# Second attention of a four-layer network: output biases moved to the projections, scales issued slot by slot, variance constant folded into the root, states copied by whole banks

## The chip, the core and the metric

The kernel runs on one core of one Trainium2 chip. The metric is the device time of one execution in microseconds; the median of three runs stands for a kernel. Five engines work beside each other, each through its own instructions in order: PE (TensorE, matrix products), DVE (VectorE), ACT (ScalarE), POOL (GpSimd) and SP, which here only issues DMAs. All data are float32.

## The reference

The network has four layers over 4096 tokens of 256 channels. Layers 0 and 1 are convolutional; layer 2 has the attention that the change touches, followed by a mixture of eight experts with two chosen for each token; layer 3 is softmax attention and again a mixture of experts. The attention of layer 2, with eight heads of h = 32 channels, is

```
q, k, v = linear(x)                                 # x: layer norm of t
sim  = sum(q * k) * qk_norm_scale
k, v = k / |k|, v / |v|
Z    = outer(v, k) * kv_norm_scale                  # h x h for each token and head
gates = square(relu(Z.flat @ wg.T + wg_b)) + 1e-5
m, s  = online softmax scan of sim                  # running maximum and sum
Z_scan, g_scan = cumsum(gates * Z), cumsum(gates)
weights = exp(sim - m) / (s + 1e-5)
attn = Z_scan / (g_scan + 1e-5) * (1 + silu(weights))
t = t + linear(q @ attn, wo_w, wo_b)
```

so the sum over earlier tokens is linear attention, and each token and head has one factor, (1 + silu(weights)) / (g_scan + 1e-5), which can be put on q. The layer norm divides by sqrt(var + 1e-5); the router of the experts works on a second layer norm of the new t.

## The kernel before

Tokens lie on the 128 partitions: 32 tiles (NT) of 128 tokens, 8 blocks (NBLK) of 4 tiles (TPB), 16 slots of 2 tiles. `attn2` (L1375) runs in three stages.

**Projections** (`attn2_project`, L1466 on), one set of steps for each block: `norm` (layer norm of t into a_n), `turn` (transposes on PE), four times `project` (products on PE, bias added by DVE at L1492 into a_qk and a_v), `lengths` (squares on ACT, sums on DVE, the product q*k on POOL at L1502), `sims`, `turn_v`, and `gates` (products with wg on PE, then a row of DVE operations L1524 to L1532, and on POOL at L1533 the keys times their gate). The loop in `attn2` calls them so that block b's gates stand beside block b+1's projections and block b+2's norm. Only PE follows that written order; the instructions of the other engines are ordered by the framework's scheduler, which takes what is ready by its own estimate of time. The projections of one block are 32 matmuls.

**Factors** (`attn2_fac`, L1560). The order of PE, DVE, ACT and POOL is written out by hand. Gates and sims are turned so that 256 values of one head and slot range lie along the free axis; the scans run on DVE; `carry` (L1592) takes the ends of the rows through two small products (a_c and a_back) to give each row its start. It is called twice, for sums and maxima and then for the softmax total. Between these, `beside(n)` issues n of the 31 products of the states (`attn2_states`, L1539): for a tile, 8 small products v by k into one of four PSUM banks (a_st_ps), and after every fourth tile a copy by ACT (L1554) of four states into SBUF and then four running sums by POOL (L1556). The total's reciprocal is L1645, Silu L1647, the reciprocal of the gates' sum L1648, both put together by L1649; PE turns the result (L1653) and DVE copies it to a_fac (L1654).

**Slots** (`attn2_sum`, L1656), also in hand-written order on four engines. For slot u: `scale` (POOL, L1671) multiplies q by the factor, `turn` (PE, copied by ACT at L1682) transposes q, `scores` (PE L1692, masked by DVE at L1695), `context` (PE: L1706 with the states of earlier tiles, L1712 within the tile; ACT L1725 copies), and `out` for the slot before (PE, then DVE adds the product to t at L1731). `bias` (POOL, L1674) adds wo_b to t. All scales and biases are queued on POOL before the loop over slots. The routing for the experts (`route_parts`, L2020 on) is woven into the loop: for four tiles each, statistics of t (DVE L212, L213), the root of the variance (`norm_parts`, `root`), `scales` (L222, L225, L2042), the normed rows (ACT L232, and POOL L2046 for one column), transposes (L2051), logits, the two best experts, places, and the scattering of rows by indirect DMAs that POOL issues (L2103). The first route has its statistics in slots 1 and 2, its root in slot 2 and its scatters in slots 6 and 7.

`norm_parts` (L201) makes the root with two instructions, which all layer norms of the attention and of the routing use:

```
nc.vector.tensor_scalar_add(r, mv[:, :, 1], eps)    # L217
nc.scalar.activation(r, r, AF.Sqrt)                 # L218
```

Of the kernel before, what the change touches and what calls it, by code (L numbers as in the profile page):

```python
# [10 lines left out]
F32 = mybir.dt.float32  # L11
# [77 lines left out]
class Net:  # L89
# [6 lines left out]
    def constants(self, pool):  # L96
        nc = self.nc
        self.ident = pool.tile([P, P], F32, tag="ident", name="ident")
        make_identity(nc, self.ident)
        self.ones_row = pool.tile([1, P], F32, tag="ones_row", name="ones_row")  # L100
        nc.gpsimd.memset(self.ones_row, 1.0)
        self.one = pool.tile([P, 1], F32, tag="one", name="one")
        nc.gpsimd.memset(self.one, 1.0)
        self.ones_col = self.one

        self.flags = pool.tile([P, 3], F32, tag="flags", name="flags")
# [94 lines left out]
    def norm_parts(self, pool, x, out, eps, on_act):  # L201
# [13 lines left out]
        def root():  # L215
            r = got["r"] = room("ln_rstd")
            nc.vector.tensor_scalar_add(r, mv[:, :, 1], eps)  # L217
            nc.scalar.activation(r, r, AF.Sqrt)  # L218
# [1156 lines left out]
    def attn2(self, t, S):  # L1375

        nc, tc = self.nc, self.tc
        with tc.tile_pool(name="a2", bufs=1) as pool:
# [16 lines left out]
            with (  # L1395
# [20 lines left out]
            A["st"] = left.enter_context(tc.tile_pool(name="a2s", bufs=1)).tile([P, NT, 2, D], F32, tag="st", name="a2_st")  # L1416
            self.attn2_fac(A)
            with (
# [12 lines left out]
                self.attn2_sum(t, A, tri, ked, wp, ps, route)  # L1431
# [33 lines left out]
    def attn2_project(self, b, t, A, wg_bd, wp, ps):  # L1465
# [47 lines left out]

        def turn_v():
# [21 lines left out]
        return {"norm": norm, "turn": turn, "lengths": lengths, "sims": sims, "turn_v": turn_v, "gates": gates,  # L1536
                **{i: call(i) for i in range(TPB)}}

    def attn2_states(self, A, ps):  # L1539
# [5 lines left out]
        def product(ti):  # L1545
# [6 lines left out]
            if ti % 4 == 3 or ti == NT - 2:  # L1552
                lo = ti // 4 * 4
                nc.scalar.copy(st[:, lo + 1 : ti + 2], banks[-1][:, lo % 8 : ti % 8 + 1])  # L1554
                for i in range(max(1, lo), ti + 1):
                    nc.gpsimd.tensor_tensor(st[:, i + 1], st[:, i + 1], st[:, i], ALU.add)  # L1556

        return [(lambda ti: lambda: product(ti))(ti) for ti in range(NT - 1)]

    def attn2_fac(self, A):  # L1560
# [5 lines left out]
        with (  # L1566
# [4 lines left out]
            states = self.attn2_states(A, ps)  # L1571

            def beside(n):
                for go in states[:n]:
                    go()
                del states[:n]
# [15 lines left out]
            def carry(ends, scan, first, fill):  # L1592
# [14 lines left out]
                beside(1)  # L1607
# [12 lines left out]
            def sums_and_tops(x, c):  # L1620
# [3 lines left out]
            c2 = carry([ends[:, 0:1], ends[:, 1:2]], sums_and_tops, (0.0, -3e38), 8)  # L1624
# [12 lines left out]
            nc.vector.tensor_scalar_add(gs, gs, 1e-5)  # L1637
            tot = pool.tile([P, L], F32, tag="tot", name="a2_tot")
# [3 lines left out]
                       (0.0,), 12)  # L1642
# [5 lines left out]
            nc.vector.reciprocal(gs, gs)  # L1648
            nc.vector.scalar_tensor_tensor(s, s, 1.0, gs, ALU.add, ALU.mult)  # L1649
            beside(len(states))  # L1650
# [3 lines left out]
            nc.vector.tensor_copy(A["fac"].rearrange("p a s h -> p a (s h)"), p)  # L1654

    def attn2_sum(self, t, A, tri, ked, wp, ps, route):  # L1656
# [15 lines left out]

        def bias(u):
            nc.gpsimd.tensor_tensor(t[:, two(u), :], t[:, two(u), :], bc(self.row("wo_b"), 1, 2), ALU.add)  # L1674
# [66 lines left out]
        with self.tc.manual_schedule(engines={ET.PE, ET.DVE, ET.Activation, ET.Pool}):  # L1741
            scale(0)
            scale(1)
            bias(0)
            turn(0)
            scores(0)
            for u in range(2, U):
                scale(u)
                bias(u - 1)
            bias(U - 1)  # L1750
            for u in range(U + 6):
                if u + 1 < U:
                    turn(u + 1)
# [1160 lines left out]
```

## Time and profile before

| | us |
|---|---|
| runs | 3508.52, 3509.21, 3514.0 |
| median | 3509.21 |
| profiled execution | 3443.01 |
| its span, first to last instruction | 3441.5 |
| layers 0 and 1, start of the second attention's loads | 0 to 1433.4 |
| projections | 1433.4 to 1570.7 |
| factors | 1570.7 to 1590.7 |
| slots, with the routing's tail | 1590.7 to 1762.3 |
| experts, third layer's attention and experts, output | 1762.3 to 3441.5 |

Busy shares of the span: PE 90%, DVE 67%, ACT 39%, POOL 42%; the mean granted clock of PE is 0.951. A line of the profile gives the start and length in us (or, for groups, the count, the busy time and the mean in ns), the engine, the line of the kernel, the operation, what it writes and reads, and in brackets how long its engine had been idle and what ended the wait. "L146" is the helper for matrix products, so the tile's name tells which product it is. Digits are left out of tile names (a2_st is a_st). The engine's order is that of its queue: an instruction that waits holds up all behind it.

### The profile page before, as it was taken

Reading aid. Unit: us, or ns where it says so; the run is one execution under the profiler, and the core shown is the slowest. Engines: PE = TensorE matmul, PEld = TensorE weight load, DVE = VectorE, ACT = ScalarE, POOL = GpSimd, SP = SyncE. Lnnn points to the kernel's source line nnn. Section 1 sums busy time; section 2 is a strip of 40 time slices with the busy share of each in tenths; the row PEclk is TensorE's granted clock in tenths of the full one; section 3 lists DMA queues with packets and bytes.
Section 4 is the critical chain, followed back from the end, with each engine's and each line's share of the span. In section 5 each row is a group of like instructions: output and inputs, shape, how many; then the busy total and the mean of one; then the engine's idle time right before and its main releaser. Section 6 shows DMA issues by size and latency. Waiting matters only on the chain.

```text
span 3441.5 us, 66218 instructions
## 1 busy us (share of the span) xinstructions
PE 3103.2 (90%) x25772; PEld 2319.7 (67%) x25772; DVE 2311.1 (67%) x5339; ACT 1327.2 (39%) x2554; POOL 1457.5 (42%) x1323
## 2 busy tenths in 40 slices
PE   6779999999977899896969789999999996999997
PEld 3443444344436888665857567888888885999996
DVE  8885777577754677796855576777777775555552
ACT  4444334444425666242633352222222222333331
POOL 2028788778843555326344352000000003555552
PEclk9889999999988999897979899999999997999998
DMA  2146556521134222100158643323333214555554
GB/s 74 40 114 142 161 154 168 130 68 52 48 116 111 68 74 73 44 1 2 52 183 264 215 181 127 98 86 98 99 99 98 91 64 154 200 194 199 206 206 176
DMA packets 241688, 407.01 MB, mean 118 GB/s; under 512 B 78353, under 2 KB 152850, under 8 KB 231890
## 3 DMA queue, kind: packets, MB, share of 16 engines
q1 hardware_dynamic: 212002, 344.40, 32.2%
q0 software_dynamic: 13056, 35.93, 2.8%
q10 hardware_dynamic: 16304, 22.31, 1.9%
q8 instruction: 207, 3.39, 0.4%
q14 instruction: 119, 0.97, 0.1%
HBM read 287.07 MB, written 111.30 MB: 116 GB/s over the span
## 4 chain that ended last, share of the span: by engine, by line
PE 42%; DVE 9%; DMA 5%; issue 5%; ACT 3%; POOL 3%; SPq 0%; POOLq 0%; DVEq 0%; ACTq 0%
PE a_sa_ps L2537 6%; PE f_h_ps L146 5%; DMA ys<-f_y,f_at 3%; PE l_acc_ps L1154 3%; PE a_oa_ps L2576 3%; PE a_ob_ps L2576 3%; PE a_oc_ps L2576 3%; PE a_sb_ps L2537 3%; PE f_ya_ps L146 2%; PE f_yb_ps L146 2%; POOL ys L2292 2%; DVE l_pr L1150 2%; PE a_od_ps L2576 1%; PE a_q_ps L146 1%; PE a_qkv_ps L146 1%
## 5 line engine op out<-in xcount | busy, mean ns | idle before, releaser
L770 ACT COPY l_sc<-l_s 128x384 f32<-128x384 f32 (+1 forms) x632 | 304.0, 532 | 456.9 <-PE l_s L763 445.0
L775 DVE TENSOR_TENSOR l_sm<-l_s,mask 128x256 f32<-128x256 f32 (+2 forms) x628 | 308.2, 552 | 89.2 <-PE l_s L763 88.0
L2103 POOL DMA_INDIRECT xs<-f_room,f_to x64 | 64.5, 1007 | 698.0 <-issue 582.4
L146 PE MATMUL f_h_ps<-f_xT,f_w 128*128 128x256 f32 x1440 | 341.1, 388 | 19.4 <-DVE f_xT L2212 9.7
L146 PEld LDWEIGHTS f_h_ps<-f_xT,f_w 128*128 128x128 f32 x1440 | 262.2, 192 | 84.0 <-ACT f_h L2222 31.3
L763 PE MATMUL l_s<-l_q,l_k 32*128 32x256 f32 (+3 forms) x2944 | 270.5, 453 | 0.0
L2556 ACT ACTIVATE a_e<-a_e 128x512 f32<-128x512 f32 x256 | 156.0, 629 | 246.2 <-DVE a_e L2526 245.2
L780 POOL TENSOR_TENSOR l_sm<-l_sc,mask 128x768 f32<-128x768 f32 (+1 forms) x116 | 201.9, 1748 | 88.2 <-ACT l_sc L770 88.1
L2222 ACT ACTIVATE f_h<-f_h_ps,f_w 128x256 f32<-128x256 f32 x360 | 166.6, 470 | 187.9 <-PE f_h_ps L146 178.7
L1150 DVE TENSOR_TENSOR l_pr<-l_vk,l_w_ps 128x1280 f32<-128x1280 f32 x128 | 186.7, 1482 | 55.2 <-PE l_acc_ps L1154 37.6
L763 PEld LDWEIGHTS l_s<-l_q,l_k 32*128 32x128 f32 x2944 | 132.4, 183 | 115.2 <-issue 67.5
L2292 POOL DMA_INDIRECT ys<-f_y,f_at x144 | 145.7, 1012 | 140.6 <-ACT f_y L2291 110.0
L1154 PE MATMUL l_acc_ps<-ident,l_pr 128*128 128x128 f32 x1600 | 198.1, 278 | 7.7 <-POOL l_pr L1145 7.6
L1154 PEld LDWEIGHTS l_acc_ps<-ident,l_pr 128*128 128x128 f32 x1600 | 184.7, 144 | 14.1 <-POOL l_pr L1145 8.3
L784 POOL TENSOR_TENSOR l_sm<-l_sc,mask 128x256 f32<-128x256 f32 (+1 forms) x220 | 184.9, 868 | 16.1 <-ACT l_sc L770 15.2
L2249 POOL TENSOR_TENSOR f_wt<-f_w 128x512 f32<-128x512 f32 x72 | 89.8, 1268 | 217.1 <-PE f_ya_ps L146 204.9
L2537 PE MATMUL a_sa_ps<-a_q,a_kt 128*128 128x256 f32 x512 | 155.6, 386 | 15.1 <-DVE a_u L2542 14.3
L2541 ACT COPY a_u<-a_sa_ps 128x256 f32<-128x256 f32 x128 | 47.6, 372 | 292.0 <-PE a_sa_ps L2537 292.0
L809 PE MATMUL l_b_ps<-l_sm,l_v 128*32 128x256 f32 (+2 forms) x2176 | 153.7, 372 | 0.0
L2537 PE MATMUL a_sa_ps<-a_qt,a_kt 128*128 128x256 f32 x512 | 152.3, 379 | 0.0
L780 POOL TENSOR_TENSOR l_sm<-l_sc,mask_c 128x768 f32<-128x768 f32 (+1 forms) x64 | 122.9, 1937 | 39.7 <-ACT l_sc L770 39.2
L2537 PE MATMUL a_sb_ps<-a_qt,a_kt 128*128 128x256 f32 x512 | 131.4, 379 | 0.0
(558 smaller groups left out, 7292.1 us busy)
## 6 DMA issues: line engine op xcount, KB each, us to landing
a_kt<-a_kd SPq DMA_DIRECT2D x128, 512.0 KB
f_w<-in_f_w SPq DMA_DIRECT2D x36, 1152.0 KB
f_w<-in_f_w SPq DMA_DIRECT2D x36, 1028.0 KB
xs<-zero SPq DMA_DIRECT2D x8, 4160.0 KB
l_vk<-vt SPq DMA_DIRECT2D x180, 128.0 KB
f_x<-xs SPq DMA_DIRECT2D x72, 260.0 KB
f_w<-in_f_w SPq DMA_DIRECT2D x36, 384.0 KB
l_rcp<-l_recd SPq DMA_DIRECT2D x48, 256.0 KB
```

Of the source, the lines that this page charges most:

```text
L146: self.nc.tensor.matmul(out, lhsT, rhs, start=(i == 0), stop=(i == len(pairs) - 1))
L763: nc.tensor.matmul(s[pair, j][:, at : at + m, :], key(hp), qs[hp], start=(z == 0), stop=(z == len(pieces) - 1))
L770: nc.scalar.copy(sc[:, j], s[1, j])
L775: nc.vector.tensor_tensor(to(pair, j, kind, at), pick(s[pair, j], kind, which), mask, ALU.mult)
L780: nc.gpsimd.tensor_tensor(out[:, :, at, :], of[:, :, which, :], bc(mask, 1, 2), ALU.mult)
L784: nc.gpsimd.tensor_tensor(to(1, j, kind, at), pick(sc[:, j], kind, which), mask, ALU.mult)
L1150: nc.vector.tensor_tensor(pr, vk, bc(held["w"][:, j, dy], 3, D), ALU.mult)
L1154: nc.tensor.matmul(acc[:, m, j, :], pf[:, dx, m * P : (m + 1) * P], self.ident, is_transpose=True, start=(j == 0 and dy == 0 and dx == 0 a ...
L2222: nc.scalar.activation(h[:, m, :], q, AF.Gelu, bias=w1[:, 2 * hidden + m : 2 * hidden + m + 1])
L2292: nc.gpsimd.indirect_dma_start(out=self.ys_parts[(i % 4) * NI + k], in_=y[:, k, :], in_offset=None, out_offset=bass.IndirectOffsetOnAxis(a ...
L2537: mm = lambda out, i, right: nc.tensor.matmul(out, A[i], right, start=True, stop=True)
L2576: nc.tensor.matmul(out, vs[:, j, i, :], right, start=(j == 0 and side != 1), stop=(j == NPAIR - 1 and side != 0))
```

## The change

- `root` is one activation, the square root of variance plus a bias that is read from a new column `self.eps` of 1e-5, which is set once at the start. L217 goes.
- The bias of the output is added in the projections, one POOL operation of 128x1024 for each block (four tiles), called after `gates`. The sixteen of 128x512 in `attn2_sum` go.
- In `attn2_sum` the scales of slots 0 and 1 are queued first and PE's turn of slot 0 stands between them; the scale of slot u+2 is queued at the start of loop pass u.
- In `attn2_fac` no products stand ahead of the small products of `carry`; sixteen tiles' products follow the first carry and fifteen the second. ACT copies whole banks (eight states, the last seven) and POOL sums eight at a time; the copies of banks 2 and 3 come after Silu, and their sums (`late`) go into the first pass over the slots, after the scale of slot 2.
- The reciprocal of the gates' sum goes into a tile of its own and is issued inside the second `carry`, after its first product.

```diff
@@ norm_parts
         def root():
             r = got["r"] = room("ln_rstd")
-            nc.vector.tensor_scalar_add(r, mv[:, :, 1], eps)
-            nc.scalar.activation(r, r, AF.Sqrt)
+            assert eps == 1e-5
+            nc.scalar.activation(r, mv[:, :, 1], AF.Sqrt, bias=self.eps[:, 0:1])
@@ attn2, attn2_project
                         go(b, "gates")
+                        go(b, "bias")
...
+        def bias():
+            nc.gpsimd.tensor_tensor(t[:, tiles, :], t[:, tiles, :], bc(self.row("wo_b"), 1, TPB), ALU.add)
@@ attn2_states
-            if ti % 4 == 3 or ti == NT - 2:
-                lo = ti // 4 * 4
-                nc.scalar.copy(st[:, lo + 1 : ti + 2], banks[-1][:, lo % 8 : ti % 8 + 1])
-                for i in range(max(1, lo), ti + 1):
-                    nc.gpsimd.tensor_tensor(st[:, i + 1], st[:, i + 1], st[:, i], ALU.add)
-
-        return [(lambda ti: lambda: product(ti))(ti) for ti in range(NT - 1)]
+
+        def copy(k):
+            n = min(8, NT - 1 - 8 * k)
+            nc.scalar.copy(st[:, 8 * k + 1 : 8 * k + 1 + n], banks[k][:, :n])
+
+        def add(k):
+            for i in range(max(1, 8 * k), min(8 * k + 8, NT - 1)):
+                nc.gpsimd.tensor_tensor(st[:, i + 1], st[:, i + 1], st[:, i], ALU.add)
+
+        def products(lo, hi):
+            for ti in range(lo, min(hi, NT - 1)):
+                product(ti)
+
+        return products, copy, add
@@ attn2_fac
-            def carry(ends, scan, first, fill):
+            def carry(ends, scan, first, wait=lambda: None):
...
-                beside(fill)
                 self.mm(p.rearrange("p j s -> p (j s)"), [(hot, R.rearrange("p j s -> p (j s)"))])
+                wait()
...
-                beside(1)
                 self.mm(p, [(hotT, x[:, :, 0:NS])])
...
-            c2 = carry([ends[:, 0:1], ends[:, 1:2]], sums_and_tops, (0.0, -3e38), 8)
+            c2 = carry([ends[:, 0:1], ends[:, 1:2]], sums_and_tops, (0.0, -3e38))
+            products(0, 16)
...
             nc.scalar.activation(dec, dec, AF.Exp)
+            for k in range(2):
+                copy(k)
+                add(k)
...
-                       (0.0,), 12)
+                       (0.0,), lambda: nc.vector.reciprocal(upto, gs))
+            products(16, NT)
...
             nc.scalar.activation(s, s, AF.Silu)
-            nc.vector.reciprocal(gs, gs)
-            nc.vector.scalar_tensor_tensor(s, s, 1.0, gs, ALU.add, ALU.mult)
-            beside(len(states))
+            nc.vector.scalar_tensor_tensor(s, s, 1.0, upto, ALU.add, ALU.mult)
+            for k in range(2, 4):
+                copy(k)
...
+        return lambda: [add(k) for k in range(2, 4)]
@@ attn2_sum
             scale(0)
+            turn(0)
             scale(1)
-            bias(0)
-            turn(0)
             scores(0)
-            for u in range(2, U):
-                scale(u)
-                bias(u - 1)
-            bias(U - 1)
             for u in range(U + 6):
+                if u + 2 < U:
+                    scale(u + 2)
+                if u == 0:
+                    late()
                 if u + 1 < U:
                     turn(u + 1)
```

More of the change, by code (lines that the diff above doesn't have):

```diff
@@ L104, in constants @@
         self.ones_col = self.one
+        self.eps = pool.tile([P, 1], F32, tag="eps", name="eps")
+        nc.gpsimd.memset(self.eps, 1e-5)
         self.flags = pool.tile([P, 3], F32, tag="flags", name="flags")
@@ L1414, in attn2 @@
                         go(b, "gates")
+                        go(b, "bias")
             left = ExitStack()
             A["st"] = left.enter_context(tc.tile_pool(name="a2s", bufs=1)).tile([P, NT, 2, D], F32, tag="st", name="a2_st")
-            self.attn2_fac(A)
+            late = self.attn2_fac(A)
             with (
@@ L1429, in route @@
                     return self.route_parts(t0, T, t, S, wp, n.rearrange("p (i c) -> p i c", c=CX), nT, bank)
-                self.attn2_sum(t, A, tri, ked, wp, ps, route)
+                self.attn2_sum(t, A, tri, ked, wp, ps, route, late)
             with (
@@ L1535, in attn2_project @@
         call = lambda i: lambda: project(i)
-        return {"norm": norm, "turn": turn, "lengths": lengths, "sims": sims, "turn_v": turn_v, "gates": gates,
+        return {"norm": norm, "turn": turn, "lengths": lengths, "sims": sims, "turn_v": turn_v, "gates": gates, "bias": bias,
                 **{i: call(i) for i in range(TPB)}}
@@ L1570, in attn2_fac @@
         ):
[L1571 to L1576, printed above, removed]
+            products, copy, add = self.attn2_states(A, ps)
             seg = pool.tile([P, NS], F32, tag="seg", name="a2_seg")
@@ L1637, in attn2_fac @@
             nc.vector.tensor_scalar_add(gs, gs, 1e-5)
+            upto = pool.tile([P, L], F32, tag="upto", name="a2_upto")
             tot = pool.tile([P, L], F32, tag="tot", name="a2_tot")
@@ L1654, in attn2_fac, with attn2_sum @@
             nc.vector.tensor_copy(A["fac"].rearrange("p a s h -> p a (s h)"), p)
-    def attn2_sum(self, t, A, tri, ked, wp, ps, route):
+        return lambda: [add(k) for k in range(2, 4)]
+    def attn2_sum(self, t, A, tri, ked, wp, ps, route, late):
         nc, w = self.nc, self.w
@@ L1671, in scale @@
             nc.gpsimd.tensor_tensor(qh, qh, bc(A["fac"][:, :, u, :], 3, D), ALU.mult)
-        def bias(u):
-            nc.gpsimd.tensor_tensor(t[:, two(u), :], t[:, two(u), :], bc(self.row("wo_b"), 1, 2), ALU.add)
         def turn(u):
```

## The prediction, made before the changed kernel ran

> **What bounds the kernel now.** I read the page first (TensorE busy 90% of the span, the chain of waits 42% on PE), then the chain of waits in order of time through the stages that the diff touches. It names PE nearly everywhere between 1590 and 1729 us, with one foreign piece, 10.63 us of "DVE ln_rstd L217". The table by stretches shows the same hole. Its columns are stretch, length, then busy time of PE, weight load, DVE, ACT and POOL, granted PE clock, DMA share and GB/s; the stretches are projections, factors, first three slots, the hole, the other slots.
>
> ```profile
> 1433.40:1570.70 137.30, 119.00 (x580) 79.41 (x580) 121.92 (x280) 54.44 (x106) 35.17 (x22) 0.92 0.04 10
> 1570.70:1590.70 20.00, 9.39 (x442) 7.90 (x442) 13.28 (x35) 6.80 (x14) 10.12 (x32) 0.50 0.02 4
> 1590.70:1613.00 22.30, 20.49 (x306) 16.04 (x306) 10.65 (x16) 4.03 (x8) 22.30 (x23) 0.78 0.01 1
> 1613.00:1625.60 12.60, 2.23 (x36) 1.87 (x36) 10.94 (x4) 1.88 (x4) 10.86 (x13) 0.68 0.00 0
> 1625.60:1729.00 103.40, 102.72 (x1533) 87.56 (x1533) 81.07 (x268) 64.93 (x123) 38.87 (x45) 0.92 0.15 51
> ```
>
> In the fourth row PE works 2.23 of 12.60 us. The timeline says why:
>
> ```profile
> 1613.02 10.62 DVE L217 TENSOR_SCALAR ln_rstd<-ln_mv 128x4 f32<-128x4 f32 x1
> 1621.46 2.14 POOL L1674 TENSOR_TENSOR t<-t,pr 128x512 f32<-128x512 f32 x2
> 1623.71 1.28 ACT L218 ACT_TABLE_LOAD   x1 [13.83 <-DVE ln_rstd L217]
> 1625.12 0.82 ACT L1725 ACTIVATE w_qkv<-a_c_ps,a_ked 128x256 f32<-128x256 f32 x2
> 1625.62 3.78 PE L146 MATMUL a_o_ps<-w_o,w_qkv 128*128 128x256 f32 x8 [10.39 <-ACT w_qkv L1725]
> 1630.19 1.55 PE L1706 MATMUL a_c_ps<-w_qkv,a_st 32*32 32x128 f32 x32
> ```
>
> An addition over four columns takes 10.62 us where the median of its line is 0.165. It ends at 1623.64, just as Pool's unbroken row of scales (L1671) and biases (L1674) ends (1621.46 + 2.14 = 1623.60). ACT's root stands behind it, ACT's L1725 behind the root, PE's output product behind L1725. Second place, the end of the factors:
>
> ```profile
> 1585.46 1.75 DVE L1648 RECIPROCAL a_gs<-a_gs 128x256 f32<-128x256 f32 x1
> 1586.39 4.34 POOL L1556 TENSOR_TENSOR a_st<-a_st 128x64 f32<-128x64 f32 x11 [3.81 <-ACT a_st L1554]
> 1588.57 0.42 DVE L1654 COPY a_fac<-a_fac_ps 128x256 f32<-128x256 f32 x1 [0.78 <-PE a_fac_ps L1653]
> 1590.69 2.05 POOL L1671 TENSOR_TENSOR a_qk<-a_qk,a_fac 128x512 f32<-128x512 f32 x2
> ```
>
> The factors are there at 1588.99, but the first scale waits for the state sums on its own engine until 1590.69, and PE with it. Third, one block of the projections, where DVE is busy 14.3 of 14.3 us and PE 14.1:
>
> ```profile
> 1505.05 2.36 POOL L1502 TENSOR_TENSOR a_room<-a_qk 128x1024 f32<-128x1024 f32 x1 [6.22 <-ACT a_room L1499]
> 1505.42 2.04 DVE L1527 TENSOR_TENSOR a_g<-a_g,a_r 128x32 f32<-128x32 f32 x1
> 1511.22 1.91 POOL L1533 TENSOR_TENSOR a_qk<-a_qk,a_g 128x1024 f32<-128x1024 f32 x1 [3.81 <-DVE a_ss L1503]
> 1511.50 1.68 DVE L1506 TENSOR_TENSOR a_r<-a_ss 128x32 f32<-128x32 f32 x1
> ```
>
> Two DVE products of 32 columns take 2.04 and 1.68 us, each until the Pool operation beside it ends (1507.41, 1513.13); with Pool idle they take 0.32 and 0.18, the minima of their lines. This is the place where the change puts more work on Pool.
>
> [...] on L217 it goes further, since the wait spans ten Pool instructions that overlap (each lasts 1.05 to 1.09 us and starts 1.00 to 1.05 after the last). [...] BN_STATS and PSUM adds beside the same Pool row (0.43 and 0.69 us) and reductions beside L1502 (1.21) kept their usual times. [...] here eight output matmuls take 3.78 us after the hole and 1.89 before it.
>
> **The root and the scales by slot.** Removed: the 24 additions of L217 (the eight of the third layer and seven of these routes hide behind PE or DVE work: nothing), and the row on Pool: 14 scales and 16 biases of 1.05 us pace, Pool busy without a gap from 1590.69 to 1623.60. After it slots 0 and 1 are scaled first, slots 2, 3, 4, 5 when they are queued (Pool then waits at L2046 of the first route for slot 1's context), so Pool is idle at the root of slot 2. Without the hole: the averages (L213) end at 1612.98, table load 1.28 and root 0.20 give 1614.5, L1725 ends at 1615.3, L1682 (0.59) at 1615.9, the four L232 (2.08) at 1618.0, the transposes of the route (0.6) at 1618.6, and slot 3's L1706 starts at about 1618.9 instead of 1630.19: 11.3 saved, and 0.5 for its cold clock (1.55 against 1.08). PE's output product fits into this at 1615.1 to 1617.0. A check: slot 4 to 5 takes 9.01 (1637.08 to 1646.09) with 1.95 of logits that slot 2 lacks, so 7 to 8 for slot 2 to 3; I have 8. I take 11.5.
>
> What it costs: a scale of 1.05 in each later slot can hold a DVE operation of the routing for up to 1.05. DVE is busy 81 of 103 us there and PE 102.7; I put 0.3 on it for the whole stage (0 to 2). PE's turn of slot u+1 needs a scale that is queued behind the row scatters of slot u-1, which wait for routing. Four scatters take 5.1 (first at 1653.94), then the scale is done at 1660.1; the turn that needs it is in the loop two slots on (1666.97 or later): over 6 us of cover, so nothing.
>
> **The factors.** Products move behind the first carry: 256 of them from 1574.7 at 15 to 18 ns (128 in 1.94, 48 in 0.87) end at 1578.6 to 1579.3, where DVE needs PE at 1579.1. The reciprocal (1.75) runs from 1579.1 to 1580.8 while PE makes the second carry, whose copy started at 1580.54: 0.3 late. It leaves the place after L1646, where only Silu (0.42, ends 1585.99) is left before L1649: from 1587.31 to 1586.05, 1.26 saved, net 1.0. Then the first scale starts on a Pool that is free (its 15 sums begin after 1577.8 and at 0.41 end by 1584.2), 1.7 saved. Fifteen sums stand after the scale of slot 2 now, 6.2 us on Pool from about 1591 to 1597; the scale behind them is needed by slot 2's turn at 1606, and their states in slot 8. The sums of the first half run beside L1639, L1643 and L1644 of DVE, which may wait 0.32 each (one sum): 0.5 in all. Gain 1.0 + 1.7 - 0.5 = 2.2 (1 to 3).
>
> **The bias.** Eight Pool operations of 128x1024, each about 2.1 (twice L1674's 1.05 pace), join 4.27 of Pool work in each 14.3 us. The bytes are no load; what counts is which DVE operation stands beside them. Only PE keeps its written order in this stage, and the trace shows the scheduler taking what is ready: L1502 of block 7 runs before L1533 of block 6, and the statistics of later blocks run at 1433 to 1454. A bias is ready when the norm of its block has read t (L232, ending at 1503.09 or 1517.39), and Pool is then idle until 1505.05 or 1519.35. There it fills 1517.4 to 1519.5 beside reductions and PSUM adds, which don't wait, and makes L1502, and so L1527, later by about 0.15 in three blocks, 0.6 and 0.5 in blocks 1 and 5. That sums to 1.5; L217's going frees about 0.1 of DVE in six blocks. Cost 1 (0 below, 17 above: see the rival).
>
> **Sum.** 11.5 + 2.2 - 0.3 - 1.0 = 12.4 us. The profiled execution took 3443.0 with a span of 3441.5, so about 3430.6 and 3429.1. The median of the runs is 66 higher; nothing in the profile says where, so I carry the difference over unscaled: 3509.2 - 12.4 = 3496.8. The end is tied to it: routing's last 24 scatters, the experts' rows and products follow in the chain without a clock of their own.
>
> **Rivals.** (1) The bias is queued straight behind L1502 or L1533, as it is written. Then Pool doesn't let go and the DVE product that waits there waits 2.1 more, with DVE full and PE at 14.1 of 14.3: 8 x 2.1 = 16.8, in place of my 1: 3509.2 - 13.4 + 16.8 = 3512.6, slower. It decides from 1.7 a block. For it: the order in the text, the pair L1533/L1506. Against: the idle gaps and the hoisted statistics. (2) Half of it: biases hit DVE in some blocks, or the sums of the factors hold DVE longer; 7 of cost in all, 3503. (3) The stall at 1613 isn't Pool's and stays, so only the factors gain: 3508. Against: the ends agree within 0.04 us, and the adder is gone anyway; what follows it on DVE are a reciprocal and L225 on a quiet Pool.
>
> **Numbers.** Forecast 0.74, rival 1 0.11, rival 2 0.10, rival 3 0.05. The likeliest's own range is 3493 to 3501 (root 10.5 to 12.5, factors 1 to 3, bias 0 to 3, scales 0 to 2). Eight in ten needs part of rival 2: 3491 to 3506. A measurement of this kernel tells 0.2%, 7 us, from no change. Faster by more: all of the forecast and a third of rival 2, 0.77; within: rivals 1 mostly, 2 and 3, 0.18; slower: rival 1 with more than 2.1 a block, 0.05.
>
> **What would show it.** No line of DVE above 2.5 us in the slots; slot 2 to slot 3 of L1706 at about 8 us; first scale within 0.2 us of the factors' copy; blocks of the projections still 14.3 apart. A DVE L1506 or L1527 of some 4 us would show rival 1; a hole at the root of slot 2, rival 3.

## The result, and the profile after

The changed kernel takes 3476.34 us in the median of four runs (3473.02 to 3479.55), the kernel before 3509.7; the ratio is 0.9903, with an interval of 0.9886 to 0.9920. That is 33 us less; the forecast was 12.4 less, with a range that ended at 3491. (Ratios and intervals here and below are those on record; they differ a little from the ratio of the two medians.)

One fact has to come first. The kernel before has two speeds, and which one it shows goes with the chip. In the six sets of runs made for this study, each on one chip, its median was 3505.7, 3507.0 and 3502.7 us in three, and 3439.7, 3443.2 and 3441.3 in the other three. Within a set all runs were of one kind. Five chips came up, and the one that came up twice was stretched both times; whether it is the chip itself, or something else that stays the same within a set, was not tested. I call the first kind stretched, the second unstretched. The runs of the result, before and after, are of the stretched kind; the profile that the prediction was read from (3443.0 us) shows the unstretched kind. So the kernel before was profiled again on a stretched chip (span 3506.1), and the change has to be read twice. The table gives both, in us; the changed kernel's own two columns are the profiles of after_c (unstretched, below) and of the result (stretched). The projections are counted here from PE's first product, a slot from its L1706 (after: L1717); the last two columns are differences, the second to the new profile.

| | before, unstretched | before, stretched | after, unstretched | after, stretched | difference, unstretched | difference, stretched |
|---|---|---|---|---|---|---|
| start of projections | 1445.6 | 1445.5 | 1441.1 | 1443.6 | -4.5 | -1.9 |
| projections, to the rows' transposes | 122.8 | 122.7 | 123.3 | 123.4 | +0.5 | +0.7 |
| factors, to the first scale | 22.2 | 22.5 | 19.8 | 19.3 | -2.4 | -3.2 |
| first scale to slot 0 | 8.6 | 8.6 | 8.6 | 8.6 | 0 | 0 |
| slots 0 to 4 | 37.8 | 37.7 | 25.4 | 25.7 | -12.3 | -12.0 |
| slots 4 to 15 | 89.8 | 142.9 | 89.8 | 128.9 | 0.0 | -14.0 |
| slot 15 to the last scatter | 35.4 | 45.5 | 35.7 | 44.2 | +0.3 | -1.3 |
| the rest | 1679.2 | 1680.6 | 1683.0 | 1681.7 | +3.8 | +1.1 |

The start of the projections and the rest are touched by the change only in the roots of their layer norms; over all profiles made here, of kernels with and without the change, they spread from 1436.7 to 1445.6 and from 1674.4 to 1684.3. What lies between them gives 13.9 us on the unstretched kind and 29.8 on the other. A second stretched profile of the changed kernel (a_look) has 126.6 us in slots 4 to 15 and 40.9 behind them, so the last column is good to some 5 us in all.

The first gain is the predicted one. The timeline of the changed kernel at the root of slot 2:

```profile
1608.65 0.18 DVE L215 BATCH_NORM_AGGREGATE ln_mv<-ln_st 128x2 f32<-128x6 f32 x1
1608.91 1.28 ACT L220 ACT_TABLE_LOAD   x1 [3.11 <-DVE ln_mv L215]
1608.96 1.05 POOL L1685 TENSOR_TENSOR a_qk<-a_qk,a_fac 128x512 f32<-128x512 f32 x1
1610.21 0.30 ACT L220 ACTIVATE ln_rstd<-ln_mv,eps 128x4 f32<-128x4 f32 x1
1610.41 0.82 ACT L1736 ACTIVATE w_qkv<-a_c_ps,a_ked 128x256 f32<-128x256 f32 x2
1614.07 1.08 PE L1717 MATMUL a_c_ps<-w_qkv,a_st 32*32 32x128 f32 x32
```

Statistics, table, root and the context's copy (L1736) follow each other without a hole. POOL has one scale here instead of a row, and slot 3 starts 7.2 us after slot 2 (1606.83), where it took 19.3. The root reads the variance itself; no DVE operation stands ahead of it.

The end of the factors in the changed kernel:

```profile
1577.97 1.75 DVE L1654 RECIPROCAL a_upto<-a_gs 128x256 f32<-128x256 f32 x1
1585.70 0.42 DVE L1667 COPY a_fac<-a_fac_ps 128x256 f32<-128x256 f32 x1 [0.53 <-PE a_fac_ps L1666]
1586.21 3.06 POOL L1685 TENSOR_TENSOR a_qk<-a_qk,a_fac 128x512 f32<-128x512 f32 x3 [2.75 <-DVE a_fac L1667]
1589.22 5.87 POOL L1565 TENSOR_TENSOR a_st<-a_st 128x64 f32<-128x64 f32 x15
```

The reciprocal has moved into the second carry, POOL has been idle for 2.75 us when the factors come, and the first scale starts 0.09 us after their copy instead of 1.70. The fifteen late sums follow behind the scale of slot 2.

The bias in the projections:

```profile
1501.59 2.01 POOL L1518 TENSOR_TENSOR t<-t,pr 128x1024 f32<-128x1024 f32 x1 [4.35 <-ACT a_n L234]
1503.55 2.36 POOL L1505 TENSOR_TENSOR a_room<-a_qk 128x1024 f32<-128x1024 f32 x1
1503.83 2.13 DVE L1533 TENSOR_TENSOR a_g<-a_g,a_r 128x32 f32<-128x32 f32 x1
1515.97 2.01 POOL L1518 TENSOR_TENSOR t<-t,pr 128x1024 f32<-128x1024 f32 x1 [4.34 <-ACT a_n L234]
```

It stands in the idle gap behind the norm (ACT L234), as forecast, and the product L1505 follows 1.96 us later. From bias to bias it is 14.38 us, and a block took 14.3.

The second gain was not forecast. The tables by stretches of the kernel before on each kind, and of the kernel after on the stretched kind, for slots 4 to 15 (stretch, length, busy time of PE, weight load, DVE, ACT, POOL, then PE's granted clock, DMA share, GB/s); first the profile that the prediction had:

```profile
1637.08:1726.90 89.82, 89.17 (x1345) 76.59 (x1344) 72.42 (x247) 58.57 (x110) 37.38 (x43) 0.94 0.16 57
```

then the kernel before on a stretched chip:

```profile
1637.00:1779.90 142.90, 120.74 (x1345) 100.14 (x1344) 74.08 (x257) 59.12 (x110) 39.69 (x45) 0.77 0.11 39
```

and the kernel after, stretched:

```profile
1620.50:1749.40 128.90, 116.91 (x1345) 97.50 (x1344) 75.91 (x251) 59.90 (x110) 47.42 (x52) 0.79 0.12 43
```

The same 1345 matmuls take 89.8 or 142.9 us, at a granted clock of 0.94 or 0.77, while DVE and ACT are busy for nearly the same time. Nearly all of the difference lies where POOL issues scatters (before: L2103, after: L2113). A pass is the time from the beginning of one slot to that of the next. Of the passes from slot 6 on, those that end in an odd slot hold them; they took 9.0 to 9.9 us unstretched (the last 7.8), 18.5 to 20.3 in the kernel before stretched, and 15.7 to 16.9 in the changed kernel (only its last is 19.5). One such pass of the kernel before on an unstretched chip:

```profile
1671.72 1.72 PE L1692 MATMUL a_s<-w_qkv,a_vT 32*128 32x128 f32 x32
1671.86 0.96 POOL L2103 DMA_INDIRECT xs<-a_qk,f_to  x1 [0.31 <-issue]
1672.87 0.81 ACT L1725 ACTIVATE w_qkv<-a_c_ps,a_ked 128x256 f32<-128x256 f32 x2
1672.93 2.36 DVE L1695 TENSOR_TENSOR a_sm<-a_s,tri 128x1024 f32<-128x1024 f32 x2 [0.46 <-PE a_s L1692]
```

The same pass on a stretched chip:

```profile
1680.48 0.71 PE L1692 MATMUL a_s<-w_qkv,a_vT 32*128 32x128 f32 x6
1681.42 0.41 PE L1692 MATMUL a_s<-w_qkv,a_vT 32*128 32x128 f32 x3 [0.23 <-issue]
1682.18 0.49 PE L1692 MATMUL a_s<-w_qkv,a_vT 32*128 32x128 f32 x4 [0.34 <-issue]
...
1684.10 0.21 POOL L2046 COPY a_qk<-out_row 128x4 f32<-128x4 f32 x1
...
1688.27 0.96 POOL L2103 DMA_INDIRECT xs<-a_qk,f_to  x1 [0.30 <-issue]
1688.34 0.84 ACT L1725 ACTIVATE w_qkv<-a_c_ps,a_ked 128x256 f32<-128x256 f32 x2 [6.63 <-remote]
...
1690.96 1.22 DVE L1695 TENSOR_TENSOR a_sm<-a_s,tri 128x1024 f32<-128x1024 f32 x1 [9.75 <-remote]
```

Thirty-two score products that take 1.72 us in one go come out in handfuls of one to six, every 0.7 to 1.5 us. They wait for nothing that the trace shows ("issue"). ACT is idle for 6.63 us before its copy, which starts with the last of the eight scatters, and DVE for 9.75 us before its mask, 1.7 us after that scatter's end ("remote": no releaser inside the core is seen; DVE also needs the late products). And a pass of the changed kernel, same kind of chip:

```profile
1688.29 1.05 POOL L1685 TENSOR_TENSOR a_qk<-a_qk,a_fac 128x512 f32<-128x512 f32 x1
...
1689.18 1.66 PE L1703 MATMUL a_s<-w_qkv,a_vT 32*128 32x128 f32 x12 [0.89 <-issue]
...
1689.35 0.84 ACT L1736 ACTIVATE w_qkv<-a_c_ps,a_ked 128x256 f32<-128x256 f32 x2 [3.49 <-PE a_s L1703]
1689.45 1.23 DVE L1706 TENSOR_TENSOR a_sm<-a_s,tri 128x1024 f32<-128x1024 f32 x1 [4.09 <-PE a_s L1703]
```

Here the scale of slot u+2 stands between four scatters and four. As it ends, about 1 us after its start, PE's remaining products go through and ACT and DVE start. They waited 3.49 and 4.09 us instead of 6.63 and 9.75. The last pass, from slot 14 to 15, has no scale left to issue: its eight scatters have only the copy of 0.20 us (L2056) between them, and it is the one that still takes 19.5 us, as before the change. So the change breaks four of the five rows that lie in these slots.

### The profile page after: what moved, and what is told of

It is laid out like the page before. It is cut to its first block, busy times and chain, and to the rows that moved or that the text cites. A ratio compares the mean times of both kernels' runs of the same rounds, so it can differ in the third digit from the quotient of the medians.

```text
span 3475.3 us, 66162 instructions
## 1 busy us (share of the span) xinstructions
PE 3129.0 (90%) x25772; PEld 2335.4 (67%) x25772; DVE 2302.7 (66%) x5315; ACT 1332.0 (38%) x2550; POOL 1457.9 (42%) x1316
## 3 DMA queue, kind: packets, MB, share of 16 engines
q0 software_dynamic: 13056, 35.93, 2.7%
## 4 chain that ended last, share of the span: by engine, by line
PE 43%; DVE 8%; DMA 5%; issue 5%; POOL 3%; ACT 3%; another core or an unknown queue 0%; SPq 0%; POOLq 0%; DVEq 0%; ACTq 0%
PE a_sa_ps L2547 6%; PE f_h_ps L148 5%; DMA ys<-f_y,f_at 3%; PE a_oa_ps L2586 3%; PE a_ob_ps L2586 3%; PE a_oc_ps L2586 3%; PE l_acc_ps L1156 3%; PE a_sb_ps L2547 3%; PE f_ya_ps L148 2%; PE f_yb_ps L148 2%; POOL ys L2302 2%; DVE l_pr L1152 1%; PE a_od_ps L2586 1%; PE a_sc_ps L2547 1%; PE a_q_ps L148 1%
## 5 line engine op out<-in xcount | busy, mean ns | idle before, releaser
L2113 POOL DMA_INDIRECT xs<-f_room,f_to x64 | 64.2, 1004 | 701.8 <-issue 588.1
L148 PE MATMUL f_h_ps<-f_xT,f_w 128*128 128x256 f32 x1440 | 341.1, 388 | 18.5 <-DVE f_xT L2222 8.0
L148 PEld LDWEIGHTS f_h_ps<-f_xT,f_w 128*128 128x128 f32 x1440 | 261.9, 192 | 83.6 <-ACT f_h L2232 20.1
L765 PEld LDWEIGHTS l_s<-l_q,l_k 32*128 32x128 f32 x2944 | 132.4, 183 | 115.2 <-issue 67.5
L786 POOL TENSOR_TENSOR l_sm<-l_sc,mask 128x256 f32<-128x256 f32 (+1 forms) x220 | 184.8, 867 | 15.3 <-ACT l_sc L772 14.5
L2259 POOL TENSOR_TENSOR f_wt<-f_w 128x512 f32<-128x512 f32 x72 | 89.8, 1266 | 218.2 <-PE f_ya_ps L148 206.6
L2547 PE MATMUL a_sa_ps<-a_q,a_kt 128*128 128x256 f32 x512 | 156.8, 388 | 17.4 <-DVE a_u L2552 16.6
```

Of the source, the lines that this page charges most:

```text
L148: self.nc.tensor.matmul(out, lhsT, rhs, start=(i == 0), stop=(i == len(pairs) - 1))
L765: nc.tensor.matmul(s[pair, j][:, at : at + m, :], key(hp), qs[hp], start=(z == 0), stop=(z == len(pieces) - 1))
L786: nc.gpsimd.tensor_tensor(to(1, j, kind, at), pick(sc[:, j], kind, which), mask, ALU.mult)
L2547: mm = lambda out, i, right: nc.tensor.matmul(out, A[i], right, start=True, stop=True)
```

## The experiments

Theory A, formed on these readings: the gain has two parts, the stall at the root (on every chip), and a row of scatters that is broken by a scale (stretched chips only). Rival B: the second part comes from something else, such as another place of the routing's chain against the attention. Some expectations say "odd slots"; they mean the passes that lead to an odd slot. The time of the kernel before in the same set is given with each result, and so the kind of chip.

**The kernel before again (b_look), unchanged.**

> The kernel before, unchanged, to see in its own profile where the 66 us lie by which its profiled execution (3443.0) was below the median of its runs (3509.7). Theory A (instructions arrive late at PE): the slots and the routing's tail, 171.6 us in the profile before, take about 235 us here, with idle time of PE put down to issue beside the row scatters, and everything ahead of 1590 us and behind the scatters within 5 us of the profile before. Theory B (a slower clock over the whole kernel): every stage is longer by about 1.9%, the slots by 3 us only.

3504.96 us against 3505.68 (0.9997, 0.9988 to 1.0006). This is the profile called stretched above. (Theory A of this expectation is another one, on how instructions reach PE; that they reach it late no run showed.) From the first scale to the last scatter it takes 234.8 us, as expected there, with PE's idle time put down to "issue". It is 64.6 us longer than the first profile, 63.2 of them between the start of slot 4 and the last scatter.

**The root alone (root_only)** on the kernel before, scales and biases left in their row.

```diff
-            nc.vector.tensor_scalar_add(r, mv[:, :, 1], eps)
-            nc.scalar.activation(r, r, AF.Sqrt)
+            nc.scalar.activation(r, mv[:, :, 1], AF.Sqrt, bias=self.eps[:, 0:1])
```

> Only the constant goes into the root; scales and biases stay in one row on Pool. Prediction's theory: the 10.6 us stall at the root of slot 2 goes only in part, since the next DVE operations there [...] L225 and L2042, meet the same row of Pool until it ends at 1623.6; root and table load come 10 us earlier and the output product with them, so the slots gain 0 to 4 us. Rival (the addition alone was the trouble): 11 us less, no DVE line above 2.5 us in the slots.

3500.33 against 3505.68 (0.9991, 0.9983 to 1.0000). Slot 2 to 3 still takes 15.6 us, 3.8 less than in b_look; 0 to 4 less was expected. The root itself is early now, but the route is held again a moment later:

```profile
1606.87 0.30 ACT L220 ACTIVATE ln_rstd<-ln_mv,eps 128x4 f32<-128x4 f32 x1
1607.42 8.98 DVE L227 SCALAR_TENSOR_TENSOR ln_shift<-ln_mv,ln_rstd 128x4 f32<-128x4 f32 x1
...
1616.28 0.33 POOL L2048 COPY a_qk<-out_row 128x4 f32<-128x4 f32 x2
1616.50 2.07 ACT L234 ACTIVATE a_qk<-t,ln_shift,ln_rstd 128x256 f32<-128x256 f32 x4 [8.12 <-POOL a_qk L2048]
```

DVE's L227 (before: L225, with a median of 0.162 us) now takes 8.98 and ends at 1616.40, just as POOL's row of scales and biases ends (1616.35), as the expectation had it. The normed rows (L234, before: L232) need its result, and start 0.10 us after it. The profile names another wait for them, of 8.12 us for a one-column copy (L2048) that is queued on POOL behind the same row. So the row would have held the route at L217, and without L217 it holds it at L227 and at this copy.

**The change without its root (after_no_root)**: the two instructions of L217 and L218 put back, all else as changed.

> The change without its root: L217 is back, the rest as changed. Prediction's theory: Pool is quiet at the root of slot 2, so L217 takes 0.2 us there and the time is that of the changed kernel within 3 us (3476). Rival (the root in one step carries the gain): about 11 us slower than the changed kernel, 3487.

3476.18 against 3505.68 (0.9927, 0.9907 to 0.9948), and the changed kernel had 3476.34 in its own set: slot 2 to 3 takes 7.3 us with the addition in place, where the kernel before takes 19.3. What removes the stall is that no row on POOL stands beside the root any more; the root in one step adds nothing that can be seen beside that.

**All scales ahead of the loop (scales_early)**, so that none stands between scatters.

```diff
+            scale(2)
+            late()
+            for u in range(3, U):
+                scale(u)
             for u in range(U + 6):
-                if u + 2 < U:
-                    scale(u + 2)
-                if u == 0:
-                    late()
```

> The changed kernel with all scales queued on POOL ahead of the loop over slots, right after the late sums, so that none stands between the scatters of an odd slot. Theory A (the odd slots are shorter after the change because a scale of 1.06 us breaks the row of eight scatters into four and four): odd slots from 6 on go back from 16.5 to about 20 us, five of them, so 3476 + 17 = about 3493 us; slot 2 to 3 stays near 7 us, since the late sums and scales end before the first router tile. Rival B (the odd slots are shorter because the router's chain now stands differently to the attention's after the stall at the root is gone): odd slots stay near 16.5 us and the time at 3476. If both the stall at slot 2 comes back (15 scales of 1.06 us in one row on POOL) and the row is whole: about 3505.

3423.08 us against 3439.70 (0.9943, 0.9925 to 0.9960): the set fell on an unstretched chip, where the kernel before has nothing to win in those passes, so the run tells nothing between A and B. It was made again.

> All scales ahead of the loop, none between scatters. Where the kernel before takes 3440 us: no difference from the changed kernel, as in the first run (3423 us). Where it takes 3505: Theory A (a scale of 1.06 us between four and four scatters is what shortens the stretched slots) says 3476 + 17 = about 3493 us with odd slots of 20 us; rival B (the router's chain only stands better) says 3476 and odd slots of 16.5.

3483.69 against 3506.96 (0.9940, 0.9922 to 0.9958), and the changed kernel in the same set 3470.42: 13 us lost. The passes with scatters are back at 18.3 to 20.1, and slots 4 to 15 take 140.2 us:

```profile
1617.50:1757.70 140.20, 118.39 (x1345) 99.99 (x1344) 72.58 (x251) 59.71 (x110) 39.82 (x45) 0.77 0.11 39
```

A holds. The sum is smaller than the 17 that I put down for five passes, because the changed kernel breaks only four rows: those four passes grow by 2.7 to 3.7 us, the last one stays at 19.3. Slot 2 to 3 stays at 7.2 although all scales stand in one row, since that row, without the biases, ends at 1605.35, 1.55 us after slot 2 begins (1603.80); in the changed kernel the table load of the root stands 2.08 us behind that beginning (1608.91 against 1606.83). So the first gain doesn't need the scales by slot once the biases are out of the row; the second does.

**The kernel before with work added to POOL (before_split)**: a 128x512 multiply of a scratch tile between four scatters and four, in the odd passes 7 to 15.

```diff
                 do(u, 4, "scatter", range(0, 2))
+                if 7 <= u < U and u % 2:
+                    nc.gpsimd.tensor_tensor(scr, scr, scr, ALU.mult)
                 do(u, 5, "scatter", range(2, 4))
```

> The kernel before with one extra POOL multiply of 128x512 on a scratch tile between the two groups of four scatters, in the odd passes 7 to 15. The stall at the root in slot 2 is left as it is. Theory A (broken row): odd slots from 6 on fall from 20 to about 16.5 us, 3505 - 5 x 3.5 = about 3488 us, although POOL does more work. Rival B: no change at the odd slots or some longer by the 1.06 us of the multiply, 3505 to 3510.

3439.80 against 3439.70 (0.9995, 0.9987 to 1.0003), again the unstretched chip: nothing won, and nothing lost. On a stretched one:

> The kernel before with an extra POOL multiply of 128x512 between four and four scatters, the stall at the root left in. Where the kernel before takes 3440 us: no difference, as in the first run. Where it takes 3505: Theory A says odd slots of 16.5 instead of 20 us and about 3488 us; rival B says 3505 to 3510.

3484.67 against 3506.96 (0.9943, 0.9925 to 0.9961): five multiplies without a use make the kernel before 22 us faster. The stall at the root is still there (slot 2 to 3 takes 19.8), the passes with scatters take 15.8 to 17.1. That includes the last one (16.6), which this multiply breaks too and which the changed kernel leaves at 19.5. The timeline shows the multiply letting the others go:

```profile
1674.51 1.04 POOL L1762 TENSOR_TENSOR a_scr<-a_scr 128x512 f32<-128x512 f32 x1
...
1675.32 1.66 PE L1692 MATMUL a_s<-w_qkv,a_vT 32*128 32x128 f32 x12 [0.45 <-issue]
```

Rival B falls: neither the routing nor the attention was moved.

**A shorter break (before_short)**: the same with a multiply of 128x128.

> The kernel before with a short POOL multiply (128x128, about 0.3 us) instead of the 128x512 one between four and four scatters. Where the kernel before takes 3505 us: if any gap in the row lets the others go, as with the 1.04 us multiply, about 3485 us and odd slots of 16 to 17; if the gap must last as long as the others need to take up their work (the 0.2 us copy that already stands there does not break the row), no change: 3500 to 3507 and odd slots of 20. Where it takes 3440: no difference.

3441.13 against 3443.17 (0.9996, 0.9990 to 1.0003), unstretched, and 3442.70 against 3441.25 in a second such set. The third set was of the stretched kind:

> The kernel before with a 128x128 POOL multiply (about 0.3 us) between four and four scatters. Where the kernel before takes 3440 us: no difference (3441 and 3443 so far). Where it takes 3505: if any gap is enough, about 3485 us and odd slots of 16 to 17; if the gap must last about 1 us, no change, 3500 to 3507 and odd slots of 20.

3497.37 against 3502.69 (0.9988, 0.9981 to 0.9994). The multiply took 0.40 us, and the row went on:

```profile
1699.06 0.20 POOL L2050 COPY a_qk<-out_row 128x4 f32<-128x4 f32 x1
1699.21 0.40 POOL L1762 TENSOR_TENSOR a_scr<-a_scr 128x128 f32<-128x128 f32 x1
...
1703.05 0.84 ACT L1725 ACTIVATE w_qkv<-a_c_ps,a_ked 128x256 f32<-128x256 f32 x2 [6.33 <-remote]
...
1705.96 2.35 DVE L1695 TENSOR_TENSOR a_sm<-a_s,tri 128x1024 f32<-128x1024 f32 x2 [9.49 <-remote]
```

ACT and DVE wait nearly as long as without it. The passes took 16.2, 18.8, 20.3, 20.3 and 20.8 us: the first two gained something, the others nothing. If it is the length that counts, it lies between 0.40 us (nearly no use) and 1.04 us (use).

**No scatters in the slots (scatters_last)**: the changed kernel with all 64 issued in one row after the loop. (They are moved here, not removed.)

> The changed kernel with all 64 scatters of the slots after the loop, as one row. Where the kernel before takes 3505 us: Theory A in its strong form (the scatters alone hold PE, DVE and ACT) says that every odd slot falls to 9 to 10 us, as where the kernel before takes 3440, and that slot 15 begins at about 1706 us instead of 1745; the experts' rows then come 64 x 1.27 = 81 us after the last slot, so the total is about 3476 - 39 + 81 less the 30 to 49 us that the scatters after the last slot take now: 3469 to 3490. If the odd slots stay above 14 us without scatters, something else of the router holds them. Where it takes 3440: slots as in the changed kernel, total up by 30 to 50 us.

3461.53 against 3441.25 (1.0057, 1.0034 to 1.0080) on an unstretched chip: 40 us lost to the changed kernel there, since the row no longer hides behind the slots. On a stretched one:

> All 64 scatters in one row after the loop over slots. Where the kernel before takes 3440 us: as in the first run, 3462 us, with slot 15 near 1706 us. Where it takes 3505: Theory A in its strong form says that the odd slots fall to 9 to 10 us and slot 15 begins near 1706 us, as on the other kind of chip, so the total is about 3462 there too, up to 10 us more for what the row still holds after the slots. If something else of the router holds the odd slots, they stay above 14 us and the total is about 3500.

3481.43 against 3502.69 (0.9948, 0.9931 to 0.9965), and the slots are those of an unstretched chip:

```profile
1613.70:1702.60 88.90, 87.92 (x1348) 75.20 (x1347) 70.76 (x230) 59.12 (x110) 11.21 (x16) 0.96 0.02 7
```

The scatters beside them are the cause of the stretching: the rest of the routing is still in these passes, and they take 9.0 to 9.9 us (the last 7.8). The total was about 20 us above the expected 3462; from slot 15 to the last scatter it took 87.0 us, on the unstretched chip 73.8.

**The changed kernel on the other kind of chip (a_look, after_c).**

> The changed kernel as it is. The kernel before has shown two speeds on two chips: 3505 us, with odd slots of 20 us, on one (call it the stretched chip), and 3440 us, with odd slots of 9 to 10 us and PE running through the scatters, on the other. Theory A (two gains: the stall at the root goes on every chip, 12 to 17 us; the odd slots shrink only where they are stretched): 3440 - 17 = about 3423 us where the kernel before takes 3440, about 3476 where it takes 3505. Rival B (one gain whose size has nothing to do with the stretching): the same 29 to 33 us on both, so about 3409 where the kernel before takes 3440.

The first of the two fell on a stretched chip: 3470.42 against 3506.96 (0.9903, 0.9887 to 0.9920), the result once more.

> The changed kernel once more, to have it beside the others of this set. Where the kernel before takes 3440 us: theory A (the stall at the root is the only gain there) says 3440 - 17 = about 3423 us, the same as with all scales ahead of the loop; rival B (the whole 33 us on every chip) says about 3408. Where it takes 3505: 3470 to 3477.

3421.21 against 3441.25 (0.9938, 0.9922 to 0.9955), which is 20 us less and not 33. Slots 4 to 15 take 89.8 us, as before the change:

```profile
1618.20:1708.00 89.80, 89.15 (x1349) 76.39 (x1348) 73.96 (x241) 59.10 (x110) 45.01 (x50) 0.94 0.16 57
```

**Scatters in groups of two (bias_between)**: the biases go back from the projections to the slots, the first eight ahead of slot 6, the others between the scatters of two tiles.

```diff
-                        go(b, "bias")
...
+                if u < 6:
+                    bias(u + 2)
...
-                do(u, 4, "scatter", range(0, 2))
-                do(u, 5, "scatter", range(2, 4))
+                do(u, 4, "scatter", range(0, 1))
+                do(u, 5, "scatter", range(2, 3))
+                if u >= 6:
+                    bias(u + 2)
+                do(u, 4, "scatter", range(1, 2))
+                do(u, 5, "scatter", range(3, 4))
```

> The changed kernel with the biases taken out of the projections and added slot by slot on POOL (128x512), the first eight ahead of slot 6, the rest between the scatters of two tiles, so that scatters stand in groups of two. Theory A: odd slots from 6 on fall below 16.5 us, to 12 to 15, so 5 x 2 to 4 = 10 to 20 us less than the changed kernel, 3456 to 3466; the projections give back 0.5. Rival B (the row's breaking is not what counts): about 3476, or a few us more where POOL's eight early adds (about 1 us each) delay the first slots.

3423.65 against 3439.70 (0.9943, 0.9926 to 0.9959) on an unstretched chip, as the changed kernel. On a stretched one:

> Biases taken out of the projections and put between the scatters of two tiles, which so stand in groups of two. Where the kernel before takes 3440 us: as the changed kernel, as in the first run (3424 us). Where it takes 3505: Theory A says odd slots of 12 to 15 us instead of 16.5 and 3456 to 3466 us; rival B says 3476 or a few us more.

3457.52 against 3506.96 (0.9867, 0.9850 to 0.9883), 13 us under the changed kernel of the same set. The passes with scatters take 10.3 to 11.2 us, less than the 12 to 15 expected, but for the last, which has no bias and no scale left and takes 19.6; those between them take 8.1 to 8.7 where the changed kernel takes about 6.9:

```profile
1675.03 0.50 PE L1706 MATMUL a_s<-w_qkv,a_vT 32*128 32x128 f32 x4 [0.25 <-issue]
1675.24 1.10 POOL L1688 TENSOR_TENSOR t<-t,pr 128x512 f32<-128x512 f32 x1
1675.78 1.23 PE L1706 MATMUL a_s<-w_qkv,a_vT 32*128 32x128 f32 x20 [0.24 <-issue]
1676.03 0.84 ACT L1739 ACTIVATE w_qkv<-a_c_ps,a_ked 128x256 f32<-128x256 f32 x2 [0.71 <-remote]
```

After two scatters PE is let go in the middle of its 32 products, and ACT waited 0.71 us. This is the fastest version that was measured on the stretched kind, and level with the changed kernel on the other.

**Finer still (split_more)**: six of eight scatters alone, with biases of 128x256 and the scale between them, and a scratch multiply in the late passes.

> As the kernel with biases between scatters, but finer: from pass 6 on a bias of 128x256 (about 0.55 us) stands after the first and after the third pair member, the scale of 128x512 between the second and third, so six of eight scatters of an odd slot stand alone; in the passes without bias and scale (14 to 21) a scratch multiply of 128x512 parts them two and two. Where the kernel before takes 3505 us: Theory A (other engines are held for as long as scatters follow one another without 1 us of other POOL work) says, if 0.55 us is enough, odd slots of 9.5 to 10.5 us instead of 11 and the slot before the last 12 to 16 instead of 19.6: 3440 to 3452 us; if 0.55 us is too short, about the 3457 of the groups of two or some us more. Where it takes 3440: about 3424.

3436.26 against 3443.17 (0.9980, 0.9970 to 0.9990), and 3437.97 against 3441.25 in a second set; both were unstretched, so what it does on the other kind isn't known. Where nothing is held it does not reach the 3424 expected, and loses 17 us to the changed kernel of the second set (3421.21): slots 0 to 15 take 122.8 us instead of 115.2, and it is 42.3 instead of 35.7 to the last scatter.

## Why the prediction was off

- **The stall at the root, 11.5.** Measured 12.0 and 12.3 in slots 0 to 4, slot 2 to 3 falling from 19.3 to 7.2 us. Right in size and, as after_no_root shows, in its cause, the row on POOL. root_only adds that the root in one step could not have done it: the row then holds L225 (8.98 us) and the copy L2046. The root took 0.30 us with its bias read from a column and 0.20 without. By what means a POOL operation holds L217, and why the same row left L1731 (0.69 us) and L212 (0.43) at their usual times, was not shown. The 0.5 for the clock is in the traces: behind the hole PE's granted clock was 0.50 during the output products (1625.62 to 1629.40) and 0.67 during L1706 (1.55 us); slot 3's L1717 takes 1.08 us in the changed kernel, at 1.00.
- **The factors, 2.2 (1 to 3).** Measured 2.4 and 3.2: the first scale no longer waits for the sums (1.70 to 0.09), and the reciprocal is hidden in the carry.
- **The bias, a cost of 1.0.** Measured 0.5 and 0.7. It stands in the gap behind the norm. Rival 1 (behind L1502 or L1533) didn't come: the longest L1509 or L1533 of the stage is 2.13 us.
- **What a scale in each later slot costs, 0.3.** On the unstretched kind 0.0 over slots 4 to 15, with no DVE operation above 1.23 us; on the stretched kind the longest is 1.74 us (L2002).
- **The sum.** On the kind of chip that the profile came from, the touched stages give 13.9 where the prediction had 12.4. The medians there differ by 20.0, with an interval from 15.5 to 27. The profiled execution of the changed kernel was the slowest of its four (3428.43, median 3421.21), so the 6 us between 13.9 and 20.0 can't be placed in a stage.
- **The step that failed** is this sentence: "The median of the runs is 66 higher; nothing in the profile says where, so I carry the difference over unscaled". The 66 us were no constant that a change leaves alone. They were the scatters holding the engines: 53.1 in slots 4 to 15 (142.9 against 89.8) and 10.1 behind slot 15. The scales by slot, which the prediction booked as a cost of 0.3 there, break four of the five rows of eight scatters, and that gave 14.0 us. The table's last column adds up so: 12.0 and 3.2 less 0.7, which is the forecast's part and 14.5, and 14.0 and 1.3 behind slot 15, which it did not have: 29.8 in the touched stages.

The prediction took its place for the scales from their order in the queue ("queued behind the row scatters"); it asked whether the scale would be late, and not what the scatters do to the others. From its profile alone the answer could not be seen, since there PE runs through the scatters. The 66 us between profile and runs were the sign.

What stays open is why a row of scatters holds the other engines on some chips. PE's products wait for no semaphore that the trace shows ("issue"), and no run told what else they wait for. The page of the kernel before on an unstretched chip and that of the changed kernel on a stretched one show no difference in the packets of queue q8, which they call "instruction" (207 packets, 0.4% of the DMA engines' time on both), and next to none in those of q0, "software_dynamic" (13056 packets, 2.8% and 2.7%). Whether POOL's work between the scatters lets the others go, or the mere pause in the row, was not tested either.

## What to carry to other kernels

When the profiled execution is quicker than the runs by more than their spread (here by 66 us, with runs 5.5 us apart), the difference may sit in a few stages, as it did here, and an edit there may cut it; look for it with a second profile before an edit is priced. A row of indirect DMAs issued by POOL is no neutral filler for that queue: where a chip was of the stretched kind, other work of about a microsecond between them, moved there from elsewhere, paid (14.0 us in slots 4 to 15 for the scales, 13 more for the biases); on the unstretched kind it won nothing (89.8 us in those slots before and after), and cutting the row too finely lost 17 us. And a long row of elementwise work on POOL should not stand beside the small DVE operations of a critical chain (L217 took 10.62 us there instead of 0.165, L225 8.98 in root_only instead of 0.162), nor ahead of a small copy that the chain needs from POOL (8.12 us of waiting for L2046 in root_only).

## What was not expected of the hardware

- On two of the five chips (three of the six sets), beside eight scatters in a row (0.96 us each, every 1.27 us) ACT stood idle for 6.6 and DVE for 9.8 us, and PE had one to six products per 0.7 to 1.5 us; on the others the same row held nobody.
- A POOL multiply of 1.04 us between them let the three engines go within about 1 us; one of 0.40 us mostly did not, and the 0.2 us copy that always stood there did not.
- PE lost more than the gaps: over slots 4 to 15 its granted clock was 0.77 instead of 0.94, and the same 1345 products were busy for 120.7 us instead of 89.2.
- Added work can pay: five multiplies without a use took 22 us off the kernel before on a stretched chip.
